# A graph network kernel on one core: TensorE's 32-column matmuls of two slots issued together

## Chip, cores and metric

One Trainium2 chip, one NeuronCore. The time of a run is its device time in microseconds (us); the kernel before has a median of 9048.95 us over 3 runs (9040.12 to 9049.22). Engines: PE is TensorE (PEld its weight loads), DVE is VectorE, ACT is ScalarE, POOL is GpSimd, SP issues the DMAs.

## What is computed

There are 16 graphs of 1024 nodes with 64 channels and a dense 0/1 adjacency matrix. Four layers follow each other, each with a residual and a layer norm. What is heavy is in the first: the adjacency is thinned by a rank rule ("dilate"), and then for every node and channel the weighted sum of three quantiles is taken over the values of the node's neighbours.

```python
adj_d = _dilate_adj(adj, mask)
agg = _weighted_nanquantile_agg(x, adj_d > 0)      # quantiles 0.25, 0.5, 0.75 over neighbours
h = relu((x + agg) @ W1 + b1); y = (h @ W2 + b2) * mask
x = layernorm(x + y)
# layer 1: three times  h = relu(norm(adj^T (h W) + b + h))
# layer 2: mean over neighbours, two weights;  layer 3: weighted mean over neighbours and itself
```

## The kernel before

**Selecting quantiles.** Each channel's node values are sorted once (a bitonic network on DVE, two graphs at a time). For a node, the k-th smallest neighbour value is found by counting: `x` matmuls (128 columns wide) count how many neighbours lie in each block of the sorted order, and a few steps of comparing and selecting turn a wanted rank into a value. There are S = 6 wanted ranks per node (lower and upper position of three quantiles).

**Units and slots.** A unit is a graph, a group of 8 channels and half of the nodes: 16 x 8 x 2 = 256 units. Each has 6 slots, one per wanted rank: 1536 slots, 96 per graph. The main loop (L1263) goes over slots y. For slot s of a unit:

- `masks` (L736, DVE): `mt` = counts not above the rank, 128x2048. `mt` has five buffers.
- `products` (L744, DVE): `pr` = mask times word, 128x4096, in a pool of two buffers.
- `words` (L754, PE): 12 matmuls of 32 columns into a PSUM tile `pw`, evicted by ACT to `qq`.
- `ranks` (L766, PE): 4 matmuls of 32 columns from `qq` into `pr_`, evicted by ACT to `nt`.
- `steps` (L775, PE): 8 matmuls of 32 columns on the mask `mt` and 4 on `nt` into `pv`, evicted by ACT to `val`. After it the mask's buffer is free.

A 32-column matmul uses a quarter of the PE array's columns; four of them side by side run at once (`quarters`, L678). The three PSUM tiles come from one pool of three banks (`ps_e`).

In iteration y the loop issues words of slot y-2, ranks of y-3 and steps of y-4 (L1286), then `masks(y+1)` and `products(y)` (L1313 to L1320), and then, in two half-slots ("places", 2y and 2y+1), background work, words and counts. The 28 matmuls of 32 columns at the head of an iteration are called a burst here.

**Counts and words.** While a unit runs, the next one's counts are made (`counts`, L701): for each of four blocks k, eight `x` matmuls into `x1`, evicted to `cc`, eight into `x2`, and one with `neg` onto `x1`; then ACT evicts `x1` and `x2` to `dw`. Their weights `xw` ("words") are made a group ahead in `words_at` (L1194): per block four parts (`word_part`: 4 matmuls `pa<-words_by,prow` and an ACT eviction `xw<-pa` 128x512) and two ends (`word_end`: an ACT pass `xw<-xw` 128x1024). `x1`, `x2` and `pa` share three PSUM banks (`ps_x`). The pool of words has six buffers; `cc` and `dw` have two each.

**Sums.** Four slots' `val` are added up by `fc` matmuls (32 columns, f32) three times per pair of units (`Sums.add`), and then stored.

**Background.** Sorting the next pair of graphs, `dilate` of the next graph, `degrees`, and the four layers of the graph before (`layers`) are generators. `Spread` (L1067) spreads their steps over places by due times and by an estimate of DVE's load. A step that uses PE ("p" in what it yields) comes at the earliest one slot after the last step that had been marked; its PE pieces are `pq` (transposes of dilate), `pm`, `pa` (64 columns, f32), `pc`, `pt`, `pw`, `ph`, `py`, `po`. They share one PSUM bank (`ps_l`), which DVE or ACT must have read before the next piece starts.

**Order.** The order on PE, DVE and ACT is the order in which the program issues: `link` (L291) chains each instruction to the one before on its engine, so every engine works strictly in this order, and what is issued behind a waiting instruction waits with it.

Of the kernel before, what the change touches and what calls it, by code (L numbers as in the profile page):

```python
# [28 lines left out]
S = 6  # L29
# [4 lines left out]
G8 = 8  # L34
# [3 lines left out]
def gnn_stack(  # L38
# [22 lines left out]
    B, N, C = x.shape  # L61
# [8 lines left out]
    sorts = ctx.enter_context(tc.tile_pool(name="sorts", bufs=2))  # L70
    dil = ctx.enter_context(tc.tile_pool(name="dil", bufs=1))
    big = ctx.enter_context(tc.tile_pool(name="big", bufs=2))
    prod = ctx.enter_context(tc.tile_pool(name="prod", bufs=2))
    wts = ctx.enter_context(tc.tile_pool(name="wts", bufs=6))
    work = ctx.enter_context(tc.tile_pool(name="work", bufs=2))
    lay = ctx.enter_context(tc.tile_pool(name="lay", bufs=1))
    strm = ctx.enter_context(tc.tile_pool(name="strm", bufs=3))
# [136 lines left out]
    for i in range(2):  # L214
        t = const.tile([P, N], F16, name=f"ranks{i}")
# [143 lines left out]
    def some_later():  # L359
        for item in waiting:  # L360
            if item:
                item.pop(0)()
        waiting[:] = [item for item in waiting if item]
# [318 lines left out]
    def word_part(gr, xw, k, part):  # L682

        xi, t = part // 2, part % 2 * 4
        pa = bank(ps_x, "pa")  # L690
        for i in range(4):
            mm(
                pa[:, ts(i, P)], prows[gr % 2][:, ts(t + i, P)],
                words_by[:, k, xi * P : xi * P + P], True, True,
            )
        half = xw[:, xi, t : t + 4].rearrange("p t m -> p (t m)")
        if xi:
            A.activation(half, pa, AF.Abs)
        else:
            A.activation(half, pa, AF.Relu, bias=1.0, scale=-1.0)  # L700

    def word_end(xw, xi):
        whole = xw[:, xi].rearrange("p t m -> p (t m)")
        A.activation(whole, whole, AF.Relu, bias=1.0, scale=-1.0)
# [86 lines left out]
    class Sums:  # L791

        def __init__(self, gi, gr):
            self.gi, self.gr, self.val = gi, gr, []

        def add(self, i):

# [101 lines left out]
    def held(g):  # L899

        tiles = []
        for i in range(6):
            t = wts.tile([P, 2, T, P], F16, tag="xw", name="xw").rearrange("p x t m -> p (x t m)")
            tiles.append(t.bitcast(F32))
        for i in range(2):
            t = big.tile([P, KC, HALF], F16, tag="cc", name="cc").rearrange("p k n -> p (k n)")
            tiles.append(t.bitcast(F32))
        for i in range(2):
            t = big.tile([P, 2, KC, HALF], F16, tag="dw", name="dw")
            t = t.rearrange("p a k n -> p (a k n)").bitcast(F32)  # L910
            tiles += [t[:, 0:N], t[:, N : 2 * N]]
        for i in range(2):
            t = prod.tile([P, 2, KC * HALF], F16, tag="p", name="pr")
            t = t.rearrange("p a k -> p (a k)").bitcast(F32)
            tiles += [t[:, 0:N], t[:, N : 2 * N]]
        for j in range(2 * T):
            nc.sync.dma_start(
                out=tiles[j], in_=adj[g, ts(j, P), :] if j < T else adjT[g, ts(j - T, P), :]
            )
        return tiles[0:T], tiles[T : 2 * T]  # L920
# [273 lines left out]
    def words_at(place):  # L1194


        nq, at = divmod(place + 6, 4 * S)
        nq += 1
        k, j = divmod(at, 6)
        if nq >= B * G8:  # L1200
            return
        if j == 0:
            words.setdefault(nq, {})[k] = wts.tile([P, 2, T, P], F16, tag="xw", name="xw")
        xi, j = divmod(j, 3)
        if j < 2:
            word_part(nq, words[nq][k], k, 2 * xi + j)
        else:
            word_end(words[nq][k], xi)

    live = {}  # L1210

# [47 lines left out]
        words_at(place)  # L1259
    _, counting = unit_of(1)  # L1260
    all_of(itertools.islice(counting, 68 // S))
    pairs_of, background, resident = {}, [], ()
    for y in range(n_units * S + S + 2):  # L1263
        Ordered.on = y < n_units * S
        u, i = divmod(y, S)
        g, z = divmod(y, SLOTS)
        running = u < n_units
        if running and z == 0:
            infos[g]["aggd"] = dram.tile([G8, P, HALF], F32, name="aggd")
            deg = small.tile([P, 3, T], F32, tag="deg", name="deg")  # L1270
            base = 2 * SLOTS * g
            if g == 0 and TURN < B:
                background.append(
                    Spread(sort_of(1, sorted_), 2 * n_sort + 12, 0, base + 2 * SLOTS + ROWS)
                )
            if g + 1 < B:
                background.append(Spread(dilate(g + 1, parts), 64, base, base + 168))
            background.append(
                Spread(degrees(g, deg), 2 * T + 2, base, base + 184)
            )  # L1280
            infos[g]["deg"] = deg

        w, t = divmod(y - 6, 2 * S)
        if 0 <= w < n_units // 2 and t == 2 * S - 1:
            pairs_of.pop(w).store()
        for lag, what in ((2, "words"), (3, "ranks"), (4, "steps")):  # L1286
            v, s = divmod(y - lag, S)
            if 0 <= v < n_units:
                val = getattr(live[v], what)(s)
                if what == "steps":  # L1290
                    if v // 2 not in pairs_of:
                        pairs_of[v // 2] = Sums(infos[all_units[v][0]], all_units[v][1])
                    late = val
                    if s == S - 1:
                        del live[v]
        w, t = divmod(y - 5, 2 * S)
        if 0 <= w < n_units // 2 and t % 4 == 3:
            pairs_of[w].add(t // 4)
        w, t = divmod(y - 4, 2 * S)
        if 0 <= w < n_units // 2:  # L1300
            pairs_of[w].val.append(late)
        q, p = divmod(y, 2 * S)
        nq = q + 1
        if running and p == 2 and nq + 1 < B * G8:
            load_rows(rows_of((nq + 1) // G8), (nq + 1) % G8)

        nu, sixth = divmod(y + 1, S)
        nu += 1
        if sixth == 0 and nu < n_units:
            _, counting = unit_of(nu)  # L1310


        v, s = divmod(y + 1, S)  # L1313
        if v < n_units:
            live[v].masks(s)
            some_later()
        v, s = divmod(y, S)
        if v < n_units:
            live[v].products(s)
            some_later()  # L1320
        for half in range(2):

            if running:
                Spread.taken = False
                place = 2 * y + half
                Ordered.now = place * PLACE
                if g % TURN and place == base + ROWS and g + 3 < B:

                    background.append(
                        Spread(  # L1330
                            sort_of((g + 3) // TURN, sorted_), 2 * n_sort + 12, place,
                            place + 4 * SLOTS,
                        )
                    )
                background = [b for b in background if b.gen is not None]
                for b in sorted(background, key=lambda b: -b.late(place)):
                    b.at(place)
                if z == 84 and half and g + 1 < B:
                    info(g + 1)
            if running:  # L1340
                words_at(2 * y + half)
            if nu < n_units:
                n = 2 * sixth + half
                all_of(itertools.islice(counting, 68 * (n + 1) // 12 - 68 * n // 12))
        if nu < n_units and sixth == S - 1:
            all_of(counting)
        if z >= SLOTS - S + 2 and g + 1 < B:
            load_rank(g + 1, z - (SLOTS - S + 2))
        if z < 2 and 0 < g < B:
            load_rank(g, S - 2 + z)  # L1350
        if z == 1 and g == B:
            resident = held(B - 1)
        if z == S and g:
            m = infos.pop(g - 1)
            after = layers(g - 1, m["aggd"], m["wd"], m["least"], m["den"], m["deg"], *resident)
            if g < B:
                background.append(Spread(after, 69, base + 2 * S, base + 2 * SLOTS - 4))
            else:
                all_of(after)


def program(shapes):

    import concourse.bacc as bacc

    nc = bacc.Bacc(
        "TRN2", target_bir_lowering=False, num_devices=1, dynamic_dma_scratch_size=4096
    )
    args = []
    for name, (shape, dtype) in shapes.items():  # L1370
        kind = "ExternalOutput" if name == "out" else "ExternalInput"
        dt = mybir.dt.from_np(dtype)
        args.append(nc.dram_tensor(f"{name}_dram", shape, dt, kind=kind).ap())
    with tile.TileContext(nc) as tc:
        gnn_stack(tc, *args)
    return nc
# [32 lines left out]
```

## Time and profile before

| | |
|---|---|
| Median of 3 runs | 9048.95 us |
| Profiled execution | 9048.66 us |
| Its span, first to last instruction | 9046.6 us |
| Granted TensorE clock, mean | 0.990 |
| Busy PE / DVE / ACT / POOL | 93% / 87% / 77% / 13% |
| First and last product | 324.9 us, 8887.0 us |

The page groups instructions as line, engine, operation, out<-in by the program's names, shapes and count, then busy us and mean ns of one, then the engine's idle time just before them and what ended most of it. PE's matmuls are pipelined, so a mean of 380 ns for a 512-column matmul is its latency and not its pitch; the pitch is read from the starts in the timeline. Nearly all instructions have the line of the recording helpers (L301 on PE, L320 on DVE and ACT), so one goes by tile names. Before the first product lies the sort of the first two graphs and the dilation of the first; after the last, the layers of the last graph.

### The profile page before, as it was taken

Reading aid. Unit: us, or ns where it says so; the run is one execution under the profiler, and the core shown is the slowest. Engines: PE = TensorE matmul, PEld = TensorE weight load, DVE = VectorE, ACT = ScalarE, POOL = GpSimd, SP = SyncE. Lnnn points to the kernel's source line nnn. Section 1 sums busy time; section 2 is a strip of 40 time slices with the busy share of each in tenths; the row PEclk is TensorE's granted clock in tenths of the full one; section 3 lists DMA queues with packets and bytes.
Section 4 is the critical chain, followed back from the end, with each engine's and each line's share of the span. In section 5 each row is a group of like instructions: output and inputs, shape, how many; then the busy total and the mean of one; then the engine's idle time right before and its main releaser. Section 6 shows DMA issues by size and latency. Waiting matters only on the chain.

```text
span 9046.6 us, 187484 instructions
## 1 busy us (share of the span) xinstructions
PE 8391.5 (93%) x78297; PEld 3647.9 (40%) x78297; DVE 7848.8 (87%) x8943; ACT 6938.2 (77%) x12546; POOL 1149.3 (13%) x930
## 2 busy tenths in 40 slices
PE   0699999999999999999999999999999999999996
PEld 0244444444444444444444444444444444444442
DVE  8899989898898989989899898998889898777763
ACT  1588878788787887878788787887878788787872
POOL 1110102111020110201011020111102011020000
PEclk9999999999999999999999999999999999999997
DMA  3112222222222222222222222222222222222121
GB/s 97 45 42 57 94 83 80 86 77 92 87 86 81 86 77 89 95 76 83 86 74 96 84 86 82 86 81 86 95 74 91 78 75 92 76 71 77 48 78 64
DMA packets 536995, 721.53 MB, mean 80 GB/s; under 512 B 203952, under 2 KB 331312, under 8 KB 536144
## 3 DMA queue, kind: packets, MB, share of 16 engines
q1 hardware_dynamic: 536144, 709.54, 24.2%
q8 instruction: 612, 10.03, 0.5%
q14 instruction: 239, 1.96, 0.1%
HBM read 606.57 MB, written 102.77 MB: 78 GB/s over the span
## 4 chain that ended last, share of the span: by engine, by line
PE 60%; DVE 21%; ACT 10%; issue 6%; POOL 2%; DMA 0%; SPq 0%; DVEq 0%; POOLq 0%; ACTq 0%
PE x L301 26%; PE pa L301 10%; PE pw L301 10%; DVE pr L320 7%; PE pv L301 6%; DVE mt L320 4%; DVE sr L320 3%; PE fc L301 3%; ACT xw L320 2%; DVE vt L320 2%; ACT qq L320 2%; DVE sv L320 1%; ACT nt L320 1%; DVE sc L320 1%; ACT val L320 1%
## 5 line engine op out<-in xcount | busy, mean ns | idle before, releaser
L301 PE MATMUL x<-vt,xw 128*128 128x512 f16 x16384 | 4159.0, 380 | 86.6 <-ACT dw L320 64.6
L320 DVE TENSOR_TENSOR pr<-mt,dw 128x4096 f16<-128x4096 f16 x1536 | 3508.5, 2284 | 1.4 <-PE pw L301 1.4
L320 DVE TENSOR_TENSOR mt<-cc,rB 128x2048 f16<-128x2048 f16 x1536 | 1873.7, 1220 | 930.0 <-PE pv L301 860.3
L301 PEld LDWEIGHTS <-xw 128*128 128x128 f16 x16384 | 1495.0, 98 | 1828.2 <-issue 548.4
L320 ACT ACTIVATE xw<-pa 128x512 f16<-128x512 f32 x2048 | 1248.8, 611 | 518.7 <-PE pa L301 516.8
L320 ACT ACTIVATE qq<-pw 128x512 f16<-128x512 f32 x1536 | 925.0, 602 | 827.7 <-PE pw L301 785.0
L320 ACT ACTIVATE dw<-x 128x512 f16<-128x512 f32 x2048 | 1117.5, 601 | 179.4 <-PE x L301 112.9
L320 ACT ACTIVATE xw<-xw 128x1024 f16<-128x1024 f16 x1024 | 1086.9, 1061 | 10.4
L301 PE MATMUL pw<-pr,red 128*32 128x512 f16 x12288 | 936.6, 381 | 40.4 <-DVE pr L320 40.3
L301 PE MATMUL pa<-words_by,prow 128*128 128x128 f16 x8192 | 803.1, 221 | 150.3 <-DMA prow<-rows 103.6
L301 PE MATMUL pv<-mt,txw 128*32 128x512 f16 x12288 | 934.4, 381 | 0.2 <-ACT nt L320 0.2
L320 ACT ACTIVATE val<-pv 128x512 f32<-128x512 f32 x1536 | 930.9, 606 | 4.2 <-PE pv L301 4.1
L301 PEld LDWEIGHTS <-prow 128*128 128x128 f16 x8192 | 559.7, 98 | 899.4 <-issue 589.0
L829 POOL TENSOR_TENSOR rstd<-var,neghalf 128x8 f32<-128x8 f32 x112 | 198.1, 1769 | 4662.9 <-DVE var L320 4662.9
L320 ACT ACTIVATE cc<-x 128x512 f16<-128x512 f32 x1024 | 611.0, 597 | 156.8 <-PE x L301 150.6
L301 PE MATMUL pw<-ranks,subr 128*32 128x512 f16 x6144 | 617.7, 392 | 0.1
L301 PE MATMUL pv<-nt,nbig 128*32 128x512 f16 x6144 | 600.7, 380 | 0.0
L320 DVE TENSOR_TENSOR sr<-sr 128x384 f16<-128x384 f16 (+8 forms) x1336 | 552.2, 443 | 8.4
L320 DVE TENSOR_TENSOR sv<-sv 128x512 f32<-128x512 f32 (+12 forms) x904 | 533.2, 630 | 0.6
L586 POOL TENSOR_SCALAR sk<-sc 128x1 f32<-128x1 f16 x128 | 115.0, 898 | 2984.0 <-DVE sc L320 2588.7
L301 PEld LDWEIGHTS <-txw 128*32 128x32 f16 x12288 | 332.0, 97 | 336.6 <-issue 7.6
L301 PE MATMUL x<-cc,neg 128*128 128x512 f16 x1024 | 389.0, 380 | 47.4 <-ACT cc L320 38.8
(3303 smaller groups left out, 8312.1 us busy)
## 6 DMA issues: line engine op xcount, KB each, us to landing
a<-adj_dram SPq DMA_DIRECT2D x360, 512.0 KB
a<-adjT_dram SPq DMA_DIRECT2D x240, 512.0 KB
da<-adj_dram SPq DMA_DIRECT2D x256, 256.0 KB
ac<-adjT_dram SPq DMA_DIRECT2D x256, 256.0 KB
aggd<-v SPq DMA_DIRECT2D x128, 256.0 KB
rB<-rd SPq DMA_DIRECT2D x96, 256.0 KB
v<-aggd SPq DMA_DIRECT2D x192, 128.0 KB
w<-wd SPq DMA_DIRECT2D x96, 128.0 KB
```

The lines of the kernel that those rows point to most:

```text
L301: link("PE", nc.tensor.matmul(*args, **kw))
L320: ins = call(*args, **kw)
L586: G.tensor_scalar(sk[:, 0:1], m, 0.5, 0.5, ALU.add, ALU.mult)
L829: nc.gpsimd.tensor_tensor(rstd, var, neghalf, ALU.pow)
```

## The change

- The 32-column work of two slots is issued together, in odd iterations only (`burst`): ranks of slots y-5 and y-4, words of y-3 and y-2, steps of y-5 and y-4, and then the `fc` sums of the pair before. Even iterations have no 32-column work but what the layers bring.
- Odd iterations issue `masks(y+1)` and then `products(y)`, even ones `products(y)` and then `masks(y+1)`. The masks still have five buffers.
- `prod` has three buffers for two, `wts` five for six. With that `words_at` is laid out anew: block 0 takes six places as before, then three places are empty, then each further block takes five places, one of which has an end and a part.
- `held`, which keeps the last graph's adjacency in freed buffers, follows the new counts. The layers of the graph before start two slots later in the same window's end; the loop ends two iterations earlier. The scratch for DMA descriptors is halved.

The diff, cut to its core:

```diff
-    prod = ctx.enter_context(tc.tile_pool(name="prod", bufs=2))
-    wts = ctx.enter_context(tc.tile_pool(name="wts", bufs=6))
+    prod = ctx.enter_context(tc.tile_pool(name="prod", bufs=3))
+    wts = ctx.enter_context(tc.tile_pool(name="wts", bufs=5))
...
-        k, j = divmod(at, 6)
-        if nq >= B * G8:
+        if nq >= B * G8 or 6 <= at < 9:
             return
+        k, j = divmod(at - 4, 5) if at >= 9 else (0, at)
...
+        work_of = ((0,), (1,), (4, 2), (3,), (5,)) if k else ((0,), (1,), (4,), (2,), (3,), (5,))
+        for part in work_of[j]:
+            if part < 4:
+                word_part(nq, words[nq][k], k, part)
+            else:
+                word_end(words[nq][k], part - 4)
...
+    def burst(y):
+
+        def slots(what, first):
+            for at in (first, first + 1):
+                v, s = divmod(at, S)
+                if 0 <= v < n_units:
+                    yield getattr(live[v], what)(s)
+
+        while stores:
+            stores.pop().store()
+        all_of(slots("ranks", y - 5))
+        all_of(slots("words", y - 3))
+        fresh = list(slots("steps", y - 5))
+        add_up()
...
-        for lag, what in ((2, "words"), (3, "ranks"), (4, "steps")):
-            v, s = divmod(y - lag, S)
-            if 0 <= v < n_units:
-                val = getattr(live[v], what)(s)
...
+        if y % 2:
+            burst(y)
...
-        v, s = divmod(y + 1, S)
-        if v < n_units:
-            live[v].masks(s)
-            some_later()
-        v, s = divmod(y, S)
-        if v < n_units:
-            live[v].products(s)
-            some_later()
+        pair = [("masks", y + 1), ("products", y)]
+        for what, at in pair if y % 2 else reversed(pair):
+            v, s = divmod(at, S)
+            if v < n_units:
+                getattr(live[v], what)(s)
+                some_later()
...
-        if z == S and g:
+        if z == (S + 2 if g < B else S - 2) and g:
...
-                background.append(Spread(after, 69, base + 2 * S, base + 2 * SLOTS - 4))
+                background.append(Spread(after, 69, base + 2 * S + 4, base + 2 * SLOTS - 4))
...
-        "TRN2", target_bir_lowering=False, num_devices=1, dynamic_dma_scratch_size=4096
+        "TRN2", target_bir_lowering=False, num_devices=1, dynamic_dma_scratch_size=2048
```

## The prediction

> **What bounds the kernel now.** I read the page first: busy shares, then the chain that ended last. PE is busy 93% of the span, the chain lies 60% on PE and 21% on DVE, and DVE itself is busy 87%. The two groups of every slot on DVE are the product (3508.5 us, 2.28 each) and the mask:
>
> ```profile
> PE 8391.5 (93%) x78297; PEld 3647.9 (40%) x78297; DVE 7848.8 (87%) x8943; ACT 6938.2 (77%) x12546; POOL 1149.3 (13%) x930
> ...
> L320 DVE TENSOR_TENSOR mt<-cc,rB 128x2048 f16<-128x2048 f16 x1536 | 1873.7, 1220 | 930.0 <-PE pv L301 860.3
> ```
>
> DVE's only large idle time stands before the mask, and what ends it is PE's `pv`: a mask waits until TensorE has read a mask buffer free. The shares are means, so I cut one graph (96 slots) into four windows; first and last quarter:
>
> ```profile
> 4609.00:4743.10 134.10, 124.44 (x1178) 53.18 (x1176) 132.71 (x152) 110.94 (x208) 28.02 (x20) 0.99 0.20 69
> ...
> 5015.50:5147.80 132.30, 131.18 (x1245) 56.47 (x1242) 106.11 (x120) 99.95 (x174) 3.30 (x2) 1.00 0.30 99
> ```
>
> Columns: window, us, then busy us of PE, PEld, DVE, ACT, POOL, then the clock. In the first quarter DVE is full (132.7 of 134.1) and PE waits; in the last PE is full (131.2 of 132.3) and DVE has 26 us spare. So a gain on PE counts in about three quarters of the time, and so does a new wait of PE. A slot takes 538.8/96 = 5.61 us.
>
> **1. The switches go (gain).** PE's timeline around two bursts:
>
> ```profile
> 2541.53 0.38 PE L301 MATMUL pv<-nt,nbig 128*32 128x512 f16 x4
> 2541.84 1.47 PE L301 MATMUL x<-vt,xw 128*128 128x512 f16 x6
> ...
> 2544.47 0.59 PE L301 MATMUL x<-vt,xw 128*128 128x512 f16 x2
> 2544.99 0.40 PE L301 MATMUL pw<-ranks,subr 128*32 128x512 f16 x4
> 2545.22 0.60 PE L301 MATMUL pw<-pr,red 128*32 128x512 f16 x8
> ```
>
> Between `x` matmuls the pitch is 0.216 us ((1.47 - 0.38)/5); the second `x` starts at 2544.68, and `pw` 0.31 later: entering 32 columns costs 0.09. Four 32-column matmuls start 3 ns apart and a group takes 0.216. The last `nbig` starts at 2541.54 and `x` 0.30 later, 0.1 more than from group to group: leaving costs 0.1. In the order of the built programs entries 128 to 32 go from 1529 to 766, exits 32 to 128 from 1122 to 577, exits 32 to 64 (the layers' `pa`) from 390 to 186, and 204 entries 128 to 64 come in, since a layers' piece in an even slot no longer follows a burst. 763 x 0.092 + 545 x 0.106 + 204 x 0.104 - 204 x 0.092 = **130 us less**. The instructions themselves are the same.
>
> **2. Six PSUM tiles on three banks.** A burst now asks for two `pr_`, two `pw`, two `pv`; the second `pw` needs the bank of the first `pr_`, so it waits for ACT's first `nt`. From the timeline: an idle ACT starts 0.43 after the last matmul of a group starts, `nt` takes 0.68, and PE goes on 0.05 after ACT ends. Free at 0.01 + 0.43 + 0.68 + 0.05 = 1.17 us; PE is there after five groups, 1.08: 0.09 us wait with ACT idle. In every third burst two `dw` evictions stand just ahead on ACT (pitch 0.48; the second ends its pitch at 0.63): 0.63 + 0.74 - 1.08 = 0.29. Mean 0.16 x 768 = **120 us more**. Bounds: 0 (a wait is no gain) to 0.5 x 768 = 380, if a 0.6 us background eviction is always ahead. The later tiles have 0.1 to 0.2 us margin. The Trainium skill (Perfetto Trace Analysis, "Matmuls") wants groups to rotate through banks so that evacuation overlaps the next group; by it alone this term would be nothing, the three banks being rotated.
>
> **3. ACT's old waits.** In graphs 2 to 13 PE waits 226 us for `dw`, `cc` and `xw`, 0.2 us a slot, 300 over the run, mostly in half-slots right behind a burst with a word eviction (0.6 or 1.06 us). Half of the bursts go and three word places beside the unit's start are empty, but the block boundary in mid-unit loses its burst as cover (0.2 to 0.4). I take **100 less**, bounds 200 less to 60 more.
>
> **4. What stands behind the mask on DVE (loss).** There are five mask buffers. Before, `masks(y+1)` waits for the burst of its own slot. After, at even y, masks y-4 to y are still held, and `masks(y+1)` waits for `steps(y-4)` in the burst of slot y+1, a slot later. All background work of slot y (dilate, sort, layers) is queued behind it on DVE, and PE's pieces for `pq`, `pc`, `pt`, `pm` wait for that one or two half-slots on. How it is now:
>
> ```profile
> 4949.00 1.22 DVE L320 TENSOR_TENSOR mt<-cc,rB 128x2048 f16<-128x2048 f16 x1
> ...
> 4950.14 2.29 DVE L320 TENSOR_TENSOR pr<-mt,dw 128x4096 f16<-128x4096 f16 x1
> ...
> 4952.35 0.68 DVE L320 TENSOR_TENSOR yn<-pc,rstd 128x512 f32<-128x512 f32 x1
> ...
> 4954.18 0.62 PE L298 MATMUL pq<-ident,vt 128*128 128x128 f16 x8
> ```
>
> `yn` ends at 4953.03, `pq` starts 1.15 us later: hidden. After, count from a double burst's first matmul. PE: 14 groups x 0.216 + 0.1 + 0.2 = 3.3 us, then 4.0 for each slot's other work (5.61 less today's burst of 1.6). DVE: the mask buffer is free after ten groups: 9 x 0.216 + 0.2 + 0.43 = 2.6; mask (pitch 1.14) to 3.7; the first background operation of the even slot, 0.6, ends at 4.3, its reader is due at 3.3: 1.0 late. The odd slot's: 3.7 + 1.6 (even slot's background: (7848.8 - 3508.5 - 1873.7)/1536) + mask 1.14 + product 2.20 = 8.6, + 0.6 = 9.2, reader due at 3.3 + 4.0 = 7.3: 1.9 late. Counted so for each such wait in the built order (durations of this trace, only the longest of a pair): before 82 us in the run, where the trace shows 84 in graphs 2 to 13 alone, so the count is rather low; after 585. Of the 503 more, 80 lie in first quarters, where PE waits anyway; of 423 I take 0.8, since a stall ahead moves the reader's due time: **340 more**. Bounds 100 to 500.
>
> **5. ACT behind the product.** A unit's first `dw` eviction overwrites what the last product of two units back reads:
>
> ```profile
> DVE mt L320 <- PE pv L301: 860.3, 595, 4.0
> ...
> ACT dw L320 <- DVE pr L320: 63.7, 23, 4.2
> ```
>
> (total us, times, longest.) Now 23 times. After: the product ends at 2.6 + 1.14 + 1.6 + 1.14 + 2.3 = 8.8, ACT is due at 3.3 + 0.3 + 14 x 0.216 + 0.4 = 7.0: 1.8 late in every unit, 1.0 where background is light. PE feels it in the half of the units where a word part has taken the third `x` bank: 128 x 1.4 = 180, less DVE's quarter and pieces waiting there already. I take **80 more**, bounds 0 to 250.
>
> **6. The clock.** A long pause is paid twice:
>
> ```profile
> 2533.40:2537.40 4.00, 0.13 (x3) 0.01 (x1) 4.00 (x4) 0.50 (x2) 3.66 (x2) 0.99 0.01 5
> 2537.40:2540.80 3.40, 3.25 (x17) 0.99 (x20) 3.33 (x5) 1.07 (x3) 3.13 (x4) 0.51 0.46 161
> ```
>
> PE pauses 4 us (for `dw`) and is granted half the clock for the next 3.4. In this trace pauses of 4 us bring this each time, of 2.4 us five times in seven, of 2.0 twice in eight. By part 4 some three more per graph pass 2.4 us: 15 x 3 x 1.5 = 68; I take **50 more**, bounds 0 to 120. The Trainium skill (TensorE: Matmul & The Clock Gate, "HAM oscillation") speaks against the change here, but only for idle gaps over about 3.4 us; by it one pause a graph would count, 22 us. The trace halves the clock at 2.4 already.
>
> **No cost.** The words' new places: same instructions, each block still done before it is read. Scratch halved: every listed DMA is SP's. `held` finds 5 + 2 + 4 + 6 = 17 tiles for 16. The layers start two slots later in a window that ends where it did. Products get a third buffer and never wait for more than the burst. SP's queue already waits behind DVE (1702 us for `m`); I expect it late with DVE and put it into the bounds.
>
> **Sum.** The profiled run took 9048.66 (span 9046.6 and 2 around it; median of the runs 9048.95). -130 + 120 - 100 + 340 + 80 + 50 = +360: **9410 us**.
>
> **Rivals.** *Hidden after all* (10%): DVE has time to spare in the last quarters, and if the readers stand later than I count, parts 4 to 6 shrink to 20 and banks to 80: -130 + 80 - 100 + 20 = 8920, between 8860 and 9030. Against it: spare time is of no use behind a mask that waits. *It cancels* (17%): waits of PE overlap, a third of part 4 is left: -130 + 120 - 100 + 110 + 30 + 20 = 9100, between 9030 and 9200; the 4% of no change (within 0.2%, 18 us, which is about what a measurement tells apart) come from here. *The banks* (8%): each burst waits for a late ACT, 0.5 us: 260 more, over 9640; it decides if ACT enters the bursts more than 0.8 us behind. Forecast, 9200 to 9640: 65%. Range 9100 to 9640: forecast, half of the cancelling case and the edge of the banks. Faster 10%, same 4%, slower 86%.
>
> **What would show it.** Right: `pq`, `pc`, `pt` on PE idle some 400 us more, released by DVE; the mask starts 2.5 us after a burst begins, background directly behind it; the second `pw` waits 0.1 to 0.3 for `nt`; clock a little under 0.990. Wrong: pieces start without idle time, or a mask starts before the burst reaches `steps`.

## The result, and the profile after

The kernel after takes **9761.02 us** (median of 4 runs, 9757.82 to 9763.96) against 9047.14 for the kernel before in runs beside it (9040.12 to 9049.22): ratio **1.0789**, 95% interval 1.0776 to 1.0801. It is slower, as forecast, but by 714 us and not by 360, and so outside the range (9100 to 9640). The profiled execution took 9763.96 (span 9761.9); the mean clock granted to TensorE fell from 0.990 to 0.970.

The page after, busy shares and the group of the masks:

```profile
PE 8512.4 (87%) x78297; PEld 3911.5 (40%) x78297; DVE 7834.4 (80%) x8943; ACT 7081.7 (73%) x12546; POOL 1076.0 (11%) x930
...
L320 DVE TENSOR_TENSOR mt<-cc,rB 128x2048 f16<-128x2048 f16 x1536 | 1862.5, 1220 | 1662.8 <-PE pv L301 1627.1
```

The instructions are as many as before. By their shares PE and DVE are both less busy (93% to 87%, 87% to 80%), and DVE's idle time in front of the mask has grown from 930 to 1663 us. First and last quarter of the same graph as in the prediction, cut at starts of products (window, us, busy us of PE, PEld, DVE, ACT, POOL, then the clock):

```profile
4988.63:5132.33 143.70, 124.84 (x1186) 56.40 (x1181) 131.28 (x148) 113.98 (x206) 18.93 (x18) 0.95 0.19 62
...
5424.61:5580.18 155.57, 142.07 (x1298) 64.93 (x1299) 108.83 (x122) 105.60 (x182) 4.11 (x2) 0.97 0.27 84
```

The same two quarters before, cut at the same products (the prediction's last window began 5.6 us later):

```profile
4609.05:4743.32 134.27, 124.61 (x1179) 53.27 (x1177) 132.88 (x153) 111.11 (x208) 28.24 (x20) 0.99 0.20 69
...
5009.91:5147.78 137.87, 136.72 (x1296) 58.86 (x1294) 109.79 (x123) 104.10 (x182) 3.30 (x2) 1.00 0.29 95
```

Before, the first quarter had 1.4 us of idle DVE; here it has 12.4. In the last quarter PE has 13.5 us idle, where it had 1.2. Neither engine is busy throughout any longer: each waits for the other in turn. Mean over graphs 2 to 13, us per quarter (24 slots), worked out from the starts of the products:

| quarter | before | DVE idle | PE idle | after | DVE idle | PE idle |
|---|---|---|---|---|---|---|
| 1 | 134.7 | 4.0 | 9.1 | 144.4 | 14.6 | 19.1 |
| 2 | 136.6 | 13.3 | 2.6 | 142.2 | 19.4 | 8.3 |
| 3 | 132.4 | 10.1 | 6.7 | 150.3 | 26.5 | 19.3 |
| 4 | 138.0 | 27.4 | 1.1 | 153.3 | 43.6 | 12.8 |

How one such turn looks. PE's timeline of a double burst (start, us, engine, line, operation):

```profile
2076.38 0.40 PE L301 MATMUL pr__24966<-qq,lead 128*32 128x512 f16 x4
...
2077.04 0.61 PE L301 MATMUL pw<-pr,red 128*32 128x512 f16 x8
2077.57 0.40 PE L301 MATMUL pw<-ranks,subr 128*32 128x512 f16 x4
```

The second `pw` comes 0.53 after the two groups ahead of it began, where two pitches are 0.43: the bank wait, 0.1 here. And what DVE and PE do behind that burst:

```profile
2078.88 1.23 DVE L320 TENSOR_TENSOR mt<-cc,rB 128x2048 f16<-128x2048 f16 x1 [1.74 <-PE pv L301]
...
2080.76 1.22 DVE L320 TENSOR_TENSOR mt<-cc,rB 128x2048 f16<-128x2048 f16 x1
...
2082.59 2.53 PE L301 MATMUL x<-vt,xw 128*128 128x512 f16 x11
2082.83 2.29 DVE L320 TENSOR_TENSOR pr<-mt,dw 128x4096 f16<-128x4096 f16 x1
...
2090.20 0.20 DVE L320 RECIPROCAL deg<-den 128x8 f32<-128x8 f32 x1
...
2090.46 0.39 PE L298 MATMUL pt<-ident,deg 128*24 128x128 f32 x1 [5.34 <-DVE deg L320]
```

The mask that the even slot has issued starts 2.50 us after the first matmul of the burst, as predicted, after 1.74 us of idle DVE. Then come the even slot's background, the second mask, some background, the product, the odd slot's background, and at the end of this queue eight small operations on `deg`, of which PE needs the last. PE's own work ends at 2085.1; `pt` waits 5.34 us. And then the clock:

```profile
2085.12:2090.46 5.34, 0.00 (x1) 0.00 (x1) 5.13 (x16) 0.59 (x2) 0.91 (x4) 0.83 0.48 147
2090.46:2097.30 6.84, 6.84 (x63) 2.84 (x67) 2.39 (x2) 4.54 (x9) 2.57 (x3) 0.63 0.01 1
```

The window of the pause, and the one behind it at a mean clock of 0.63. In the loop there are 100 stretches of half clock, 474 us together, where there were 21 of 89 us. Waits that grew (total us, times, longest):

```profile
DVE mt L320 <- PE pv L301: 1627.1, 525, 7.3
...
ACT dw L320 <- DVE pr L320: 196.0, 104, 6.3
...
PE pc L301 <- DVE y L320: 108.0, 50, 4.3
...
PE pt L298 <- DVE deg L320: 78.0, 15, 5.8
...
PE pw L301 <- ACT nt L320: 68.5, 104, 4.4
```

Before, the first two were 860.3 and 63.7 us (rows in the prediction), the third was this, and there was none of the last two:

```profile
PE pc L301 <- DVE y L320: 11.9, 14, 3.1
```

**An account of PE.** For graphs 2 to 13 I took every start-to-start distance on PE, set off the pitch of that shape (with the switch, where there is one), and put the rest to what ended the wait, or to half clock. The view above counts only idle time of over 0.15 us behind the modelled end of a matmul; the account also finds the many short waits, so its figure for `nt` is larger. All in us:

| graphs 2 to 13 | before | after | e1 | e9 | e10 | e12 |
|---|---|---|---|---|---|---|
| matmuls and switches | 6125.6 | 6024.4 | 6023.2 | 6017.2 | 6124.0 | 6012.7 |
| `pw` or `pv` waits for ACT's `nt` | 1.2 | 143.3 | 138.3 | 205.2 | 1.2 | 30.7 |
| waits for ACT's `dw`, `cc`, `xw` | 225.8 | 228.4 | 202.9 | 265.7 | 274.2 | 296.7 |
| `pw` waits for DVE's `pr` | 29.7 | 43.2 | 20.8 | 20.0 | 43.9 | 62.6 |
| background pieces wait for DVE | 83.6 | 467.7 | 251.7 | 112.7 | 35.4 | 119.1 |
| half clock | 32.6 | 168.7 | 115.2 | 67.3 | 30.5 | 86.7 |
| rest | 1.2 | 5.4 | 9.6 | 0 | 0 | 0 |
| sum | 6500 | 7081 | 6762 | 6688 | 6510 | 6609 |

The 12 graphs give +581 of the run's +714, so a difference in this table times 1.23 is about its share of the run.

### The profile page after: what moved, and what is told of

Its sections match the earlier page's. It is cut to its first block, busy times and chain, and to the rows that moved or that the text cites. A ratio compares the mean times of both kernels' runs of the same rounds, so it can differ in the third digit from the quotient of the medians.

```text
span 9761.9 us, 187455 instructions
## 1 busy us (share of the span) xinstructions
PE 8512.4 (87%) x78297; PEld 3911.5 (40%) x78297; DVE 7834.4 (80%) x8943; ACT 7081.7 (73%) x12546; POOL 1076.0 (11%) x930
## 4 chain that ended last, share of the span: by engine, by line
PE 50%; DVE 27%; ACT 12%; issue 8%; POOL 1%; DMA 1%; SPq 0%; POOLq 0%; DVEq 0%; ACTq 0%
PE x L301 20%; PE pa L301 8%; PE pw L301 8%; DVE pr L320 7%; PE pv L301 7%; DVE mt L320 6%; ACT dw L320 4%; ACT xw L320 3%; DVE sr L320 3%; DVE vt L320 2%; DVE sc L320 2%; DVE sv L320 2%; PE fc L301 2%; ACT nt L320 2%; ACT vt L320 1%
## 5 line engine op out<-in xcount | busy, mean ns | idle before, releaser
L301 PE MATMUL x<-vt,xw 128*128 128x512 f16 x16384 | 4208.7, 386 | 137.2 <-ACT dw L320 114.6
L301 PEld LDWEIGHTS <-xw 128*128 128x128 f16 x16384 | 1536.5, 99 | 1827.5 <-issue 513.0
L320 ACT ACTIVATE xw<-pa 128x512 f16<-128x512 f32 x2048 | 1220.8, 598 | 785.9 <-PE pa L301 785.2
L301 PE MATMUL pw<-pr,red 128*32 128x512 f16 x12288 | 957.0, 386 | 49.6 <-DVE pr L320 48.4
L301 PE MATMUL pv<-mt,txw 128*32 128x512 f16 x12288 | 954.7, 381 | 0.0
L320 ACT ACTIVATE qq<-pw 128x512 f16<-128x512 f32 x1536 | 852.1, 610 | 75.8 <-PE pw L301 72.0
L829 POOL TENSOR_TENSOR rstd<-var,neghalf 128x8 f32<-128x8 f32 x112 | 220.9, 1973 | 4902.7 <-DVE var L320 4902.7
L586 POOL TENSOR_SCALAR sk<-sc 128x1 f32<-128x1 f16 x128 | 161.5, 1262 | 3550.8 <-DVE sc L320 2467.9
L301 PEld LDWEIGHTS <-txw 128*32 128x32 f16 x12288 | 397.7, 97 | 273.7 <-issue 9.9
L301 PEld LDWEIGHTS <-red 128*32 128x32 f16 x12288 | 342.3, 98 | 326.5 <-issue 98.5
```

Source lines behind the costliest of these rows:

```text
L301: link("PE", nc.tensor.matmul(*args, **kw))
L320: ins = call(*args, **kw)
L586: G.tensor_scalar(sk[:, 0:1], m, 0.5, 0.5, ALU.add, ALU.mult)
L829: nc.gpsimd.tensor_tensor(rstd, var, neghalf, ALU.pow)
```

## Experiments

My theory after the result: what the prediction named, background queued on DVE behind a mask that waits, is most of the loss, and the half clock that follows each long pause most of the rest. Rivals: the double bursts themselves (banks, ACT's evictions), the new places of the words, or a clock that costs nothing because DVE sets the pace there.

| run | us | ratio to before, 95% interval | clock |
|---|---|---|---|
| e1_late_masks | 9366.0 | 1.0349 (1.0334 to 1.0365) | 0.977 |
| e2_before_four_masks | 11625.7 | 1.2846 (1.2827 to 1.2866) | 0.919 |
| e3_before_words_anew | 9060.3 | 1.0012 (1.0002 to 1.0021) | 0.988 |
| e4_fill_pauses | 9806.8 | 1.0837 (1.0819 to 1.0855) | 0.976 |
| e5_late_masks_lag2 | 9276.9 | 1.0257 (1.0240 to 1.0274) | 0.980 |
| e6_late_masks_lag3 | 9375.3 | 1.0364 (1.0348 to 1.0379) | 0.971 |
| e7_before_lag2 | 9130.8 | 1.0095 (1.0080 to 1.0110) | 0.984 |
| e8_fill_other_bank | 9677.3 | 1.0700 (1.0684 to 1.0716) | 0.982 |
| e9_late_masks_room | 9268.5 | 1.0243 (1.0229 to 1.0257) | 0.984 |
| e10_before_room | 9050.7 | 1.0004 (0.9995 to 1.0013) | 0.989 |
| e11_room_fc_between | 9293.1 | 1.0271 (1.0257 to 1.0285) | 0.979 |
| e12_room_four_banks | 9163.2 | 1.0125 (1.0108 to 1.0142) | 0.980 |

**e1_late_masks: the queue taken apart, all else of the change kept.**

```diff
-        pair = [("masks", y + 1), ("products", y)]
-        for what, at in pair if y % 2 else reversed(pair):
+        pair = [("products", y)]
+        if y % 2:
+            pair = [("masks", y), ("masks", y + 1)] + pair
+        for what, at in pair:
```

> The kernel after, with one edit of order: the mask of the next odd slot is no longer issued at the end of the even iteration, where it waits for the next burst with the even slot's background queued behind it on DVE, but at the head of the odd iteration, straight behind the burst. Buffers, banks, bursts and words stay. Theory (pieces of PE wait for background that stands behind a waiting mask, and each long pause costs clock after it): pauses of PE that DVE's background ends (pq, pc, pt, pm, po) fall from 531 us to under 250, half-clock windows in the loop from 100 to under 50, and the time from 9761 to about 9350 (9150 to 9450). Rival (the bursts themselves cost it, by banks and late evictions, or the new places of the words do): within 60 us of 9761.

9366 us: one edit of order gives back 395 of the 714 us. Its waits:

```profile
DVE mt L320 <- PE pv L301: 1189.4, 442, 6.3
...
PE pc L301 <- DVE y L320: 37.8, 27, 3.1
```

`pc` waits 38 us in place of 108. In the account pieces fall from 468 to 252 and half clock from 169 to 115, while the bank wait stays (143 to 138): the same bursts, cheaper. Of the half-clock stretches 62 are left (under 50 expected), and the pauses that the expectation counts (531 us) are still 288 (under 250 expected). The rival is out for this part of the loss. Some 320 us over the kernel before stay.

**e2_before_four_masks: a queue behind the mask without double bursts** (`mt` with `bufs=4` for 5 in the kernel before).

> The kernel before, with four mask buffers for five and nothing else. A mask now waits for steps that are issued one slot later, with product and background of its slot behind it on DVE: the suspected queue without any double burst. Theory: the mask's buffer comes free 2.0 us after the next burst's start, mask 1.14 and product 2.2 come first, so background ends its first operation about 5.9 us in, while its reader on PE is due at 1.6: about 4 us late; with some 40 to 80 such pieces in each of 16 graphs, 10200 to 11500 us, clock under 0.97. Rival (standing behind a mask costs little, since DVE has 13% to spare): under 9300.

11625.7 us, over the upper end. The mask's group:

```profile
L320 DVE TENSOR_TENSOR mt<-cc,rB 128x2048 f16<-128x2048 f16 x1536 | 1877.7, 1222 | 3457.0 <-PE pv L301 3403.0
```

DVE idles 3457 us before masks for 930, and in graphs 2 to 13 pieces wait 1166 us (84 before) and half clock costs 611 (33). One buffer too few, with background behind the waiting mask, is enough to make PE and DVE work in turns; no double burst is needed for it. It is a stronger case than the change, since the product stands behind the waiting mask too: `pw` waits 321 us for `pr` in the run, for 40 before.

**e3_before_words_anew: the pools and the words' places alone** (these hunks of the change's diff on the kernel before).

> The kernel before with the pools and places of the change alone: three product buffers, five of words, the words' new places, the last graph's held tiles to match, descriptor scratch halved. Single bursts in every iteration as before. Theory: the same instructions at other places, three of them empty where the counts begin: within 40 us of 9047. Rival (the words' places, with an end and a part in one half-slot, hold up PE): 100 us slower or more.

9060.3 us, 0.1% slower. In graphs 2 to 13 waits for `dw`, `cc` and `xw` fall by 30 us and `pw` waits 28 longer for `pr`. The words' places by themselves are not the cause.

**e4_fill_pauses and e8_fill_other_bank: is half clock paid for?** Matmuls that nothing reads are put ahead of three pieces (shown as in e8; in e4 they wrote to the piece's own bank):

```diff
+    def fill(n):
+
+        spare = bank(ps_e, "spare")
+        for _ in range(n):
+            matmul(
+                spare, lhsT=ident16, rhs=words_by[:, 0:2].rearrange("p k w -> p (k w)"),
+                start=True, stop=True,
+            )
...
+        fill(16)
         pt = bank(ps_l, "pt")
         transpose(pt[0 : 3 * T, 0:P], deg.rearrange("p i t -> p (i t)"), ident)
```

> The kernel after with work added: 42 matmuls of 128x512 per graph that nothing reads, into the bank that the piece behind them then overwrites: 16 ahead of the transpose of deg, 10 ahead of the first pc, 16 ahead of the turn of x3, the places of the longest pauses (5.3, 3.6, 4.7 us a graph in the mean). They fill pauses and cost nothing where the pause is longer than they are (16 x 0.216 = 3.5 us, 10 x 0.216 = 2.2 us). Theory (half clock follows the pause and costs time): some 35 of 100 half-clock windows go, 4.8 us each at about half worth, so 40 to 110 us less: 9650 to 9720. Rival (where these windows lie DVE sets the pace and the clock costs nothing): 9755 or more, and up to 9850 if the filling is in the way.

9806.8 us, which by the numbers is the rival. But the trace shows that the experiment missed: at `pc` and `x3` the pause stood before the filling, which waited for the bank; only at `deg` did it fill the pause (5.2 to 2.0 us). So it was mended:

> e4_fill_pauses mended: there the filling for pc and for the turn of x3 stood in the bank of the piece, which the same DVE operation frees that makes the piece's input, so it ran behind the pause (26 matmuls, 90 us in the run) and not in it. Now all 42 go to a bank of the bursts, before the piece asks for its own. Theory (half clock costs time): the pauses of deg, first pc and x3 shrink under 2.4 us, half-clock windows fall from 100 to 60 to 75, and the time is 9660 to 9720. Rival (the clock costs nothing where DVE sets the pace): 9750 or more.

9677.3 us: 84 less than the kernel after, with 672 matmuls more (145 us of PE's time). The pause of `deg` in the same graph, with filling, and the clock while it lasts and behind it:

```profile
2080.59 3.62 PE L301 MATMUL spare<-words_by,ident 128*128 128x512 f16 x16
...
2086.09 0.28 PE L298 MATMUL pt<-ident,deg 128*24 128x128 f32 x1 [1.88 <-DVE deg L320]
```

```profile
2080.59:2085.90 5.31, 3.61 (x17) 1.47 (x15) 5.10 (x16) 0.76 (x3) 0.73 (x3) 1.00 0.43 148
2086.08:2092.90 6.82, 6.69 (x78) 3.28 (x79) 4.50 (x4) 6.12 (x12) 2.58 (x3) 1.00 0.01 1
```

Half clock near `deg` goes from 14 stretches to one; in the loop 60 are left of 100. In the account the filling costs 108 us, the pauses shrink by 94, and half clock by 85: what is gained is the clock. So half clock is paid for, also in the first quarter, where DVE has the most work: that quarter shrinks from 144.4 to 142.1 us in the mean of graphs 2 to 13.

**e5, e6, e7: pieces later than DVE.**

```diff
-                Spread.closed = place + 1
+                Spread.closed = place + 2
...
-        yield PE
+        yield "3" + PE
         pt = bank(ps_l, "pt")
```

(e6: 3 and 4; e7 has the first edit alone, on the kernel before.)

> The kernel of e1_late_masks (9366 us), where PE's pieces of the background come at the earliest two half-slots behind the DVE work that blocks them, for one before, and the transposed deg three half-slots behind its eight DVE operations, for none. Theory (what is left over the kernel before is mostly pieces that are due before DVE is through with mask, mask and product): pauses that DVE's background ends fall from 288 us to about 120, half-clock windows from 62 to about 30, time 9050 to 9250, middle 9130. Rival (the rest is the banks, dw and the bursts, and pieces are a symptom): 9320 or more.

> As e5_late_masks_lag2, with three half-slots for two (and four for deg). Theory: nearly no such pause is left, 30 to 80 us, and the time is that of the kernel before, less the switches (130), more the banks (120 and less): 9000 to 9150, middle 9070; if the steps no longer fit their windows and are forced at its end, those pieces come together and it is slower than e5_late_masks_lag2. Rival (banks, dw and bursts): 9320 or more.

> The kernel before, with the same lag of two half-slots for one. Theory: it has 82 us of such pauses and 21 half-clock windows, mostly of dw and so not touched; 30 to 70 us of pauses go: 8980 to 9030. Rival (those pauses lie where DVE sets the pace, or the later pieces push others together): 9045 or more.

9276.9, 9375.3 and 9130.8 us: e5 just over its range (with 49 half-clock stretches for about 30 expected), e6 over its own, e7 the rival's side. The windows say why. First and last quarter of a graph in e6:

```profile
4774.58:4904.24 129.66, 116.55 (x1119) 53.17 (x1109) 127.10 (x142) 109.62 (x199) 21.33 (x18) 0.97 0.20 67
...
5170.93:5340.79 169.86, 146.81 (x1329) 68.47 (x1327) 114.48 (x134) 106.03 (x183) 4.92 (x3) 0.92 0.24 79
```

The first quarter is shorter than in the kernel before (134.3), in part because some of DVE's background has moved out of it (127.1 us busy for 132.9); the last is 32 us longer (137.9): the steps no longer fit their windows and come together at the end, PE waiting at each, as the expectation of e6 had named. e7 does the same to the kernel before (last quarter 147 us for 138).

**e9 and e10: room for the lag, with and without double bursts.**

```diff
+            lag = 2 if late < 4 else 1 if late < 8 else 0
...
-                place > Spread.closed and Spread.owner is None and not (
+                place > Spread.closed + lag and Spread.owner is None and not (
...
-                background.append(Spread(dilate(g + 1, parts), 64, base, base + 168))
+                background.append(Spread(dilate(g + 1, parts), 64, base, base + 176))
...
-                if z == 84 and half and g + 1 < B:
+                if z == 88 and half and g + 1 < B:
```

(and the layers' window ends at `base + 2 * SLOTS + 8` but for the last graph; e9 also has `"4" + PE` at `deg`).

> The kernel of e6_late_masks_lag3 with room for the lag: it is three half-slots only while the generator is less than 4 places behind its due time, two below 8 and one beyond; dilate may take until slot 88 for 84, and the layers may run 12 places longer, into the next graph. In e6_late_masks_lag3 three quarters of a graph took 396.7 us (before 403.7) and the last 168 (before 138), where steps forced at the window's end came together. Theory (the queue behind the masks is the loss, the bursts themselves gain a little): the first three quarters as there, the last 138 to 146, so 535 to 543 us a graph for 541.6 and 9250 us of e5 shrink to 8950 to 9080, middle 9010; half-clock windows under 40. Rival (the double burst costs as much as it saves in the last quarter, where PE is full): 9130 or more.

> The kernel before, with the same lag, the same room for dilate and the layers, and nothing else: what the lag alone is worth without double bursts. By e7_before_lag2 the first three quarters take 400.0 us for 403.7 and the last 147 for 138, by steps forced together. Theory: that goes, 536 to 541 us a graph, so 8950 to 9040 us, middle 9010. If pairing the bursts is worth anything net (130 of switches less 120 of banks), e9_late_masks_room is not slower than this by more than 20 us. Rival (pairing costs more than it gives): e9_late_masks_room is 60 us or more behind.

e10 takes 9050.7 us (1.0004, no difference), e9 9268.5: e9 misses its range, and the rival of both holds. With the same lag and room the double bursts are 218 us behind, though the queue is mostly gone (e9 also keeps the words' places of the change, worth 13 us in e3). The account names the difference, in 12 graphs: matmuls and switches 107 less, waits for `nt` 204 more, pieces 77 and half clock 37 more, the others 32 less. The wait for `nt` is 0.36 us a burst in the mean (205.2/576). One of the longer ones:

```profile
4814.54 0.60 PE L301 MATMUL pw<-pr,red 128*32 128x512 f16 x8
4816.02 0.40 PE L301 MATMUL pw<-ranks,subr 128*32 128x512 f16 x4 [0.88 <-ACT nt L320]
```

So this wait alone costs more than all the switches that the change saves. My theory had not expected that.

**e11 and e12: is it the bank?** e11 moves the `fc` sums between the two `pw`; e12 gives the bursts a fourth bank:

```diff
-        all_of(slots("words", y - 3))
+        pw = slots("words", y - 3)
+        next(pw, None)
+        add_up()
+        all_of(pw)
         fresh = list(slots("steps", y - 5))
-        add_up()
```

```diff
-    ps_e = ctx.enter_context(tc.tile_pool(name="ps_e", bufs=3, space=bass.MemoryType.PSUM))
-    ps_f = ctx.enter_context(tc.tile_pool(name="ps_f", bufs=1, space=bass.MemoryType.PSUM))
+    ps_e = ctx.enter_context(tc.tile_pool(name="ps_e", bufs=4, space=bass.MemoryType.PSUM))
...
-            if i == 0:
-                self.fc = bank(ps_f, "fc")
+            self.fc = bank(ps_e, "fc")
...
-                mm(self.fc[32 * j : 32 * j + 32], fin[:, f0 : f0 + 32], val, i == 0, i == 2, j)
+                mm(self.fc[32 * j : 32 * j + 32], fin[:, f0 : f0 + 32], val, True, True, j)
```

> e9_late_masks_room with the fc sums of every second burst (8 f32 matmuls, 0.95 us) moved from its end to between the words of the first and the second slot, where the second pw waits for the bank that ACT frees with nt. Theory (the bank wait is real time, 0.16 us a burst): in half of the bursts it is covered, 40 to 70 us less than e9_late_masks_room. Rival (another wait follows at once: steps for nt, or ACT): within 20 us of it.

> The kernel of e9_late_masks_room (9268 us) with four banks for the tiles of the bursts in place of three: the bank of the fc sums is given up, and each of the three fc additions goes into a tile of that pool and starts anew, so what this kernel leaves out is the adding up of the three (only the third is stored); it has the same instructions. In e9_late_masks_room the second pw waits for nt 0.36 us in nearly every burst, 205 us in graphs 2 to 13, where half of the switches' gain is 50 us. Theory (the bank): these waits go, some 150 to 250 us less, 9020 to 9120, and with that the pairing is worth about as much as it costs. Rival (ACT is full around a double burst, six evictions in 3.3 us, and only the place of the wait is the bank, as in e11_room_fc_between, where a covered wait came back at dw and cc): 9200 or more, with dw and cc waits up by what nt loses.

e11: 9293.1 us, 25 slower than e9: waits for `nt` fall from 205 to 112 us, those for `dw`, `cc` and `xw` rise from 266 to 342. The theory had 40 to 70 less; it is as the rival says, another wait follows at once, though 25 us is a little beyond its 20 too. e12: 9163.2 us, 105 less, between the two expectations. The waits at `pw` for `nt` are gone, 31 us are left at `pv` in graphs 2 to 13; of its waits in the run:

```profile
PE x L300 <- ACT cc L319: 77.4, 58, 4.9
PE pw L300 <- DVE pr L319: 75.5, 53, 5.9
```

(51.3 and 29.1 us in e9; the lines are one up, a line of the pools being gone.) In 12 graphs the waits for `nt` lose 174 us, and the other rows win 100 back. So somewhat under half of that wait was the bank; the rest came back at `dw`, `cc`, `pr` and the clock. That ACT, with six evictions to do in some 3.3 us of burst, is what holds it there agrees with e11, but was not tried by itself. None of these versions beats the kernel before.

## Why the prediction was wrong

The direction and the mechanism held; the sizes did not. The step that failed is the discount in part 4, which put the waits of first quarters at nothing, and with it the number and length of the half-clock stretches in part 6; the two terms are 130 and 117 us too small, the banks 55. "Measured" is the account's difference times 1.23.

| term | forecast | bounds | measured |
|---|---|---|---|
| 1 switches | -130 | | -125 |
| 2 banks | +120 | 0 to 380 | +175 |
| 3 and 5 ACT's waits | -100 and +80 | -200 to +60, 0 to 250 | +3, and +17 at `pr` |
| 4 behind the mask | +340 | 100 to 500 | +470 |
| 6 clock | +50 | 0 to 120 | +167 |
| rest | | | +5 |
| sum | +360 | | +712 |

- **Part 4** failed in its last step, "of the 503 more, 80 lie in first quarters, where PE waits anyway; of 423 I take 0.8". The count of 503 was close to the 470. Split by quarters, the account has about 83 of its 384 us in first quarters, some 100 over the run, and they came on top: the old waits there, for `dw`, `cc` and `xw`, did not shrink (137 us before, 138 after, in 12 graphs). The other quarters have some 370 for the 340, so the factor 0.8 was nearly right. A mask that waits leaves DVE idle, and in a first quarter DVE has the most work: its idle time there went from 4.0 to 14.6 us, and the quarter became 9.7 us longer. With the queue taken apart (e1), the first two quarters together take 275.2 us, where they took 271.3 before and 286.6 after; they are read together, since e1 moves some of DVE's background from the first to the second. The longest pauses (`pt` for `deg`, 5.3 to 5.8 us) lie in the first quarter.
- **Part 6** is the term furthest off in proportion, and the only one of the costs beyond its bounds. "Some three more per graph pass 2.4 us" at 1.5 us each; there are five more half-clock stretches per graph (100 for 21 in the loop), and 39 of the 100 are 6.8 us long. The shares read from before held: in the traces of after and five of the experiments pauses over 3.5 us always brought half clock, and those of 2 to 3 us about every second time. Too low were the number of pauses and their length: I took 1 to 2 us late for pauses that come up to 5.8. That the discount of part 4 is the reason for the number is likely, but not shown.
- **Part 2** held as a mechanism; a second `pw` waits 0.25 us in the mean of all bursts (143.3/576) for 0.16, and 0.27 where it waits (534 of them). I had ACT late by two `dw` in a third of the bursts, and it is late more often. That the three banks are rotated did not hide the wait. e12 shows that the bank is only part of it.
- **Parts 3 and 5** nearly cancel, as forecast, but neither size was right: `cc` waits 14 us less and `dw` 17 more in 12 graphs.
- The rival of the banks (each burst waits 0.5 us for a late ACT) gave the right region over 9640 for a wrong reason: `nt` cost 0.25 us a burst and not 0.5, and most of the rest is part 4. What the range should have had is a coupling: part 6 follows from the pauses of part 4, so that both come out high together. Even their two upper bounds (500 and 120) give only 9640; the bound of part 6 was itself too low.
- What was to be seen: the mask 2.5 us behind the burst (2.50), background behind it, pieces idle some 400 us more, ended by DVE (449 more in the loop, counting pauses over 0.2 us), the second `pw` waiting 0.1 to 0.3, the clock under 0.990: all there, the last by more than "a little".

What stays open: how much of the 470 and how much of the 167 would go if only the one could be taken away. e8 takes out half clock at a few places only, and e1 moves both. What holds the double bursts back once the queue is mostly gone (e9 against e10, 218 us) is named by the account, but only the bank was tried by itself (e12).

## What to carry to other kernels

Where engines work strictly in order, ask of each instruction that will wait later than before what is queued behind it, and who waits for that; a wait for a buffer in front of other engines' work can make two full engines work in turns (e2: 28% for one buffer). Do not discount such waits because the engine waits anyway: here the new waits of first quarters came on top of the old ones. And a saving on one engine (switches, 125 us) has to be held against what joining the work does to the engines that follow it: here the waits for `nt` in the double bursts alone took more than that back (175 us), somewhat under half of it by the banks in e12, and for the rest the six evictions at once on ACT are the likely but untried reason.

## What the runs showed of the hardware

The clock's stretches in all traces are whole multiples of 3.413 us on a fixed grid (their edges lie within 0.5% of a grid step). I took PE's busy time (with the modelled ends of its matmuls) in each grid window from the first product to the last, in all 14 traces: after windows at full clock with under 1.3 us of work the next one was at half clock in 855 of 855 cases; from 1.3 to 1.6 us in 159 of 373; above 1.6 us in 22 of 34185. Back to full it went only after a window at half clock with over 2.5 us of work: never below (0 of 406), in 32 of 97 from 2.5 to 2.8, and in 1003 of 1016 above. So the clock goes by the work of a whole window and not by one pause. In the traces of after, e1, e5, e6, e8 and e9, of the pauses that began at full clock, those over 3.5 us always brought half clock (128 of 128), those of 2 to 3 us about every second time (145 of 254), those of 1 to 1.5 us seldom (29 of 581), and a window with further waits stays at half clock, which is how 6.8 us come about.

The Trainium skill (TensorE: Matmul & The Clock Gate, "What's actually happening") gives a free-running window of 3413 ns, which these traces confirm. It has the clock halved after an idle window; if that means a window without work, these traces do not agree: windows with over a third of work (1.2 of 3.4 us) did it too.
